# Column scans of a four-layer convolution kernel: inputs copied to contiguous lines by GpSimd, biases added when results are kept, a longer lead of one chain over the other

## The chip, the core and the metric

The kernel runs on one core of a Trainium2 chip. The metric is device time in microseconds (us) of one execution. The engines of the core work beside each other, each through its own queue in order: TensorE (PE in the profile; its weight loads are PEld), VectorE (DVE), ScalarE (ACT), GpSimd (POOL) and SyncE (SP), which issues nearly all transfers between main memory and the on-chip memory SBUF. Matmul results arrive in PSUM, which VectorE and ScalarE read.

## The reference

The input is 4 images of 48 channels and 256 x 256 pixels. Four residual layers follow each other, each on a group-normalised input: an attention layer, a gated layer, and two equal scan layers. The change is in the scan layers:

```python
def step(w, b):
    def f(carry, inp):
        nxt = inp + _conv1d(carry, w, b)
        return (nxt, nxt)
    return f
xs = jnp.moveaxis(x, 2, 0)
d0 = xs[0]
_, d_rest = jax.lax.scan(step(down_w, down_b), d0, xs[1:])
...
x = x + _L2_conv_ref(_gn(x), ...)
x = x + _L3_conv_ref(_gn(x), ...)
```

A layer makes four scans over the whole image: down over the rows, up over the rows (with the same weights, over what down gave), right over the columns and left over the columns. One step takes the line computed before, convolves it with 5 taps over all 48 channels, adds a bias and adds the next line of the scan's input. So each step needs the result of the step before it: 255 steps a scan, four scans a layer, two layers. At the end the layer's input is added to the result of left.

## The kernel before

**Tiling of the scans.** The four images make two pairs. Each pair is one *chain* (`chain`, from L1015), a generator that yields after each step. Two neighbouring pixels of a line and 48 channels fill 96 partitions; the 5 taps become three 96 x 96 matrices (j = 0, 1, 2). A line of one image is then 128 elements on 96 partitions. The newest line is the *carry*, a tile of 96 x 2 x 130 with one image in each half; four such tiles are used in turn (`NC`, L1018).

**One step** (`step`, L1037 to L1056). For each of the two images: three matmuls on the old carry into one PSUM bank (L1045), then one VectorE add of PSUM and the input line into the new carry, then `after`, which is the scan's `keep`. In the row scans (`split` true) the add is a plain one (L1049), and input and result stand in rows cut into blocks of 8 columns. In the column scans it is a `scalar_tensor_tensor` (L1053) that adds PSUM, the bias (a column of `b_sb`) and `inp`. The float32 matmul appears in the profile as two records, so that a step has 12 records on PE, 2 adds on VectorE and 2 keeps.

**Where lines lie.** A *slot* is 16 KB a partition; each pair has five, used in rotation (L996, L1012). A slot of columns holds 16 columns (`CB`) of both images in the view of `cols_view` (L1061): batch, q, h, 8 columns. One column there, `col = cols_view(column)[:, :, w % 2, :, w // 2]` (L1225), is 128 elements with a distance of 8 elements between them.

**The scans of a layer** (`layer_of`, L1080):
- down (L1113): rows from `x`, normalised by ScalarE (L1102); keep adds the bias for the next use on ScalarE (L1125) and writes the row back; blocks of 32 rows go out to `D`.
- up (L1141): blocks come back from `D`; keep is a ScalarE copy in place (L1166); results go out to `U`, laid out by column blocks (L1198).
- right (L1216): a block of 16 columns comes from `U` one block ahead (L1221); the first column is copied to the carry (L1231); keep is a ScalarE copy into the same column (L1228); the finished block goes out to `R` (L1236).
- left (L1244): blocks come back from `R` (L1249), with the layer's input `x` in a slot `stage` (L1250); keep is a GpSimd add of the carry to `stage` (L1258), and `stage` goes out (L1267). In the first scan layer VectorE takes statistics of the finished `stage`, 8 `bn_stats` for a block of 16 columns, one after each step of the next block (`late`, L1271); they give the next layer's normalisation.

**Order of the two chains.** The loops at the end of `scans` (L1349 to L1373) write chain 0 alone for `lead` yields, then both in turn until chain 0 has ended, then chain 1 alone. `LEAD` is 3 H = 768 (L27). While chain 1 is alone, `to_rows` (L1313) brings the finished output back to rows in pieces: one piece every 24 yields for pair 0, then, in the last 128 yields, one every 10 for half of pair 1. A piece is either a set of loads (L1324) or copies on GpSimd (L1340) and ScalarE (L1344) with a store (L1346). The framework's scheduler makes the final order of each engine's queue when the program is built, from that order, from priorities and from what its own timing expects to be ready. So instructions of chain 1 may be laid down earlier than the loops write them. An engine works its queue strictly in that order.

Of the kernel before, what the change touches and what calls it, by code (L numbers as in the profile page):

```python
# [19 lines left out]
P = 96  # L20
# [3 lines left out]
RT = 32  # L24
KC = 8
NK = W // (2 * KC)
LEAD = 3 * H  # L27
F = 8
GN_EPS = 1e-5
LN_EPS = 1e-5  # L30
# [934 lines left out]
def scans(ctx, tc, xs, out, wts, biases, dram, k, coefs, lead, spare):  # L965
# [49 lines left out]
    def chain(pair):  # L1015
# [8 lines left out]
        def slot(name):  # L1024
            return take(pair, f"{name}{pair}")
# [4 lines left out]
        def advance():  # L1030
            at[0] = (at[0] + 1) % NC
            return inner()

        def blocks(v):
            return v.rearrange("p b (k w) -> p b k w", w=KC)

        def step(layer, way, inp, after, split):  # L1037

            old = carry[at[0]]
            new = advance()  # L1040
            for i in range(2):
                b = slice(i, i + 1)
                ps = sums[pair].tile([P, 512], F32, tag="bank", name=f"ps{pair}{i}")[:, : W // 2]
                for j in range(3):
                    nc.tensor.matmul(  # L1045
                        ps, lhsT=w_sb[layer][:, way, j, :], rhs=old[:, i, j : j + W // 2], start=j == 0, stop=j == 2
                    )
                if split:
                    nc.vector.tensor_add(  # L1049
                        new[:, i].rearrange("p (k w) -> p k w", w=KC), ps.rearrange("p (k w) -> p k w", w=KC), inp[:, i]  # L1050
                    )
                else:
                    nc.vector.scalar_tensor_tensor(  # L1053
                        new[:, i], ps, b_sb[layer][:, way : way + 1], inp[:, i], ALU.add, ALU.add
                    )
                after(new, b)  # L1056

        def rows_view(t):
# [1 line left out]

        def cols_view(t):  # L1061
            return t.rearrange("p (b q h w) -> p b q h w", b=2, q=2, w=KC)

        def row(ts, r):
            return rows_view(ts[r % 2])[:, :, :, r // 2, :]
# [14 lines left out]
        def layer_of(layer, first):  # L1080
# [32 lines left out]
            for n in range(NT):  # L1113
                ahead_ = None
                for r in range(RT):
                    if r == 0 and n + 1 < NT:
                        ahead_ = [slot("dn"), slot("dn")]
                        load_rows(layer, n + 1, ahead_, 0, NK)
                    if ahead_ and r >= RT // 2 and r % 4 == 0:
                        i = (r - RT // 2) // 4  # L1120
                        norm(ahead_, i // 2, i % 2)
                    inp = row(now, r)

                    def keep(new, b):
                        nc.scalar.activation(inp[:, b], blocks(new[:, b]), AF.Identity, bias=bias[:, 0:1])  # L1125

                    if n == 0 and r == 0:
                        keep(inner(), slice(0, 2))
                    else:
                        step(layer, 0, inp, keep, True)  # L1130
# [10 lines left out]
            for n in reversed(range(NT)):  # L1141
                ahead_ = None
                for r in reversed(range(RT)):
# [19 lines left out]
                    place = row(now, r)  # L1163

                    def keep(new, b):
                        nc.scalar.copy(place[:, b], blocks(new[:, b]))  # L1166

                    if i == H - 1:
                        keep(inner(), slice(0, 2))
                    else:  # L1170
                        step(layer, 0, place, keep, True)
                    yield
                    if n == 0 and r < 2:

# [7 lines left out]
                if n == 0:  # L1182

                    def keep(new, b):
                        nc.scalar.copy(last[:, b], new[:, b])

                    step(layer, 0, blocks(last), keep, True)
                    yield
                    for q in range(2):
                        nc.sync.dma_start(cols_view(column)[0:C, :, q, 0, :], last[q * C : (q + 1) * C, :, 0:KC])  # L1190
# [18 lines left out]
                now = ahead_  # L1209


            for _ in range(3):
                yield
            x, y = xs[layer][pair], xs[layer + 1][pair]
            stage = None
            for n in range(NK):  # L1216
                ahead_ = None
                for w in range(CB):
                    if w == 0 and n + 1 < NK:
                        ahead_ = slot("col")  # L1220
                        nc.sync.dma_start(by_batch(ahead_), block_of(U, n + 1))  # L1221
                    if w == 0 and n + 1 == NK:
                        stage = slot("stage")
                        nc.sync.dma_start(by_batch(stage), block_of(x, n))
                    col = cols_view(column)[:, :, w % 2, :, w // 2]  # L1225

                    def keep(new, b):
                        nc.scalar.copy(col[:, b], new[:, b])  # L1228

                    if n == 0 and w == 0:  # L1230
                        nc.vector.tensor_copy(advance(), col)  # L1231
                    else:
                        step(layer, 1, col, keep, False)
                    yield
                if ahead_ is not None:
                    nc.sync.dma_start(Rt[n], column)  # L1236
                    column = ahead_


# [4 lines left out]
            for n in reversed(range(NK)):  # L1244
                ahead_ = None
                for w in reversed(range(CB)):
                    if w == CB - 1 and n > 0:
                        ahead_ = slot("col"), slot("stage")
                        nc.sync.dma_start(ahead_[0], Rt[n - 1])  # L1249
                        nc.sync.dma_start(by_batch(ahead_[1]), block_of(x, n - 1))  # L1250
                    if layer == 0 and n == 0 and w == CB // 2:
                        following = [slot("dn"), slot("dn")]
                        load_rows(1, 0, following, 1, NK)
                    col = cols_view(column)[:, :, w % 2, :, w // 2]
                    to = cols_view(stage)[:, :, w % 2, :, w // 2]

                    def keep(new, b):
                        nc.gpsimd.tensor_add(to[:, b], to[:, b], new[:, b])  # L1258

                    if n == NK - 1 and w == CB - 1:  # L1260
                        keep(inner(), slice(0, 2))
                    else:
                        step(layer, 2, col, keep, False)
                    if late:
                        late.pop(0)()
                    yield
# [12 lines left out]
                                    cols_view(stage)[r * C : (r + 1) * C, :, q, :NH, :].rearrange("c b h w -> c b (h w)"),  # L1279
                                )  # L1280
                if ahead_:
                    column, stage = ahead_
            if layer == 0:

                ends = []
# [74 lines left out]
    for _ in chains[1]:  # L1360
        i += 1
        if i < lead - W // 2:
            if i % 24 == 0:
                next(pieces, None)
        elif i == lead - W // 2:
            for _ in pieces:
                pass
            pieces = to_rows(1, NK // 2, NK // 2, [0])
        elif i % 10 == 0:
            next(pieces, None)  # L1370
# [127 lines left out]
```

## Time and profile before

| | |
|---|---|
| median of 3 runs | 9303.49 us (9290.49 to 9321.5) |
| profiled execution, own time | 9302.44 us |
| its span, first to last instruction | 9300.7 us |
| PE busy | 8807.2 us, 95% of the span |
| PE weight loads | 7274.7 us, 78% |
| DVE busy | 4378.6 us, 47% |
| ACT busy | 3355.6 us, 36% |
| POOL busy | 1454.7 us, 16% |
| moved by DMA | 1440.82 MB, mean 155 GB/s |
| granted TensorE clock, mean | 0.975 of full speed |

All times below are counted from the span's start. The span has five stretches, by where the adds of each chain start and end in the trace:

| stretch | us |
|---|---|
| attention and gated layer, with the first steps of pair 0 from 3239 | 0 to about 3520 |
| pair 0 alone: down, up, right and the start of left (with a few steps of pair 1) | to about 4650 |
| both pairs interleaved | to 7942 |
| pair 1 alone in the second scan layer: up, right (8303 to 8694), left (8694 to 9137) | to 9137 |
| last output pieces | to 9301 |

A group line of the profile gives the source line, the engine, the operation, result and inputs, size and count, then busy time and mean duration, then the engine's idle time just before and what ended it. Matmuls are pipelined and their ends are modelled, so a PE that is busy all the time may still be slower than it could be; how many matmuls a window holds shows that.

### The profile page before, as it was taken

What the parts mean: (1) busy time and instruction counts of PE and PEld (TensorE: products, weight loads), DVE (VectorE), ACT (ScalarE), POOL (GpSimd) and SP (SyncE); (2) the same over time, 40 slices, a digit from 0 to 9 for tenths busy, and PEclk for the clock granted to TensorE, in tenths of its full rate; (3) what the DMA queues carried; (4) which work ended last, traced back from release to release, by engine and by line L of the source; (5) the groups of instructions that cost most, each with busy time, mean ns of one, the idle gap of its engine ahead of it and who ended that gap; (6) DMA issues with size and microseconds to landing.
All of it is one profiled execution on the core that took longest, in us unless ns stands there. A gap on an engine that the chain in (4) does not pass through costs nothing.

```text
span 9300.7 us, 160515 instructions
## 1 busy us (share of the span) xinstructions
PE 8807.2 (95%) x62920; PEld 7274.7 (78%) x62920; DVE 4378.6 (47%) x10798; ACT 3355.6 (36%) x7053; POOL 1454.7 (16%) x2866
## 2 busy tenths in 40 slices
PE   6999999989999889999999999999999999999982
PEld 5777777433333349999899999999999999989971
DVE  3331010335555564445666544555677555445541
ACT  0010000124334456545433465555333433445200
POOL 0000000001111120000133200000333333100462
PEclk9999999999999989999999999999999999999996
DMA  7653322568888868656477675654776787698899
GB/s 153 131 128 81 78 62 65 111 140 176 179 177 186 179 152 161 141 132 174 121 177 180 141 162 130 158 142 126 195 187 174 166 192 180 136 215 193 206 217 194
DMA packets 1058039, 1440.82 MB, mean 155 GB/s; under 512 B 64976, under 2 KB 981200, under 8 KB 991232
## 3 DMA queue, kind: packets, MB, share of 16 engines
q1 hardware_dynamic: 1057184, 1430.23, 67.5%
q8 instruction: 493, 8.08, 0.4%
q14 instruction: 266, 2.18, 0.1%
q0 software_dynamic: 96, 0.33, 0.0%
HBM read 837.19 MB, written 534.77 MB: 148 GB/s over the span
## 4 chain that ended last, share of the span: by engine, by line
PE 87%; DMA 6%; DVE 2%; SPq 2%; ACT 1%; issue 1%; POOL 1%; ACTq 0%; DVEq 0%; POOLq 0%
PE ps L1045 57%; PE py L581 6%; PE acc L294 5%; PE acc L295 5%; PE acc L296 4%; PE py L590 3%; DMA tok<-x 1%; PE pt L276 1%; DMA oi<-x 1%; PE ptok L751 1%; PE pout L868 1%; DMA col<-R 1%; PE ph L698 1%; ACT x1n L541 1%; DMA sx<-in_x 1%
## 5 line engine op out<-in xcount | busy, mean ns | idle before, releaser
L1045 PE MATMUL ps<-carry,w 96*96 96x128 f32 x48960 | 5585.1, 275 | 95.2 <-DVE carry L1053 63.3
L1045 PEld LDWEIGHTS ps<-carry,w 96*96 96x96 f32 x48960 | 5446.1, 163 | 239.5 <-DVE carry L1053 95.9
L1053 DVE SCALAR_TENSOR_TENSOR carry<-ps,b,col 96x128 f32<-96x128 f32 x4080 | 1778.1, 439 | 1129.3 <-PE ps L1045 963.1
L1258 POOL TENSOR_TENSOR stage<-stage,carry 96x128 f32<-96x128 f32 (+1 forms) x2044 | 1054.9, 520 | 3809.4 <-DVE carry L1053 3629.4
L1228 ACT COPY col<-carry 96x128 f32<-96x128 f32 x2040 | 859.9, 425 | 979.6 <-DVE carry L1053 979.0
L1125 ACT ACTIVATE dn<-carry,b 96x128 f32<-96x128 f32 (+1 forms) x2044 | 790.7, 399 | 1064.7 <-DVE carry L1049 1062.1
L1049 DVE TENSOR_TENSOR carry<-ps,dn 96x128 f32<-96x128 f32 x2280 | 651.6, 287 | 748.9 <-PE ps L1045 582.4
L1049 DVE TENSOR_TENSOR carry<-ps,up 96x128 f32<-96x128 f32 x1792 | 516.5, 288 | 657.9 <-ACT up L1166 493.9
L1166 ACT COPY up<-carry 96x128 f32<-96x128 f32 x1792 | 530.8, 298 | 584.0 <-DVE carry L1049 567.1
L581 PE MATMUL py<-x1n,wy 128*96 128x512 f32 x1536 | 700.8, 605 | 29.6 <-ACT x1n L541 27.9
L295 PE MATMUL acc<-xs,xt 128*96 128x288 f32 x2048 | 667.2, 408 | 0.0
L294 PE MATMUL acc<-xt 128*96 128x288 f32 x2048 | 666.8, 409 | 0.0
L581 PEld LDWEIGHTS py<-x1n,wy 128*96 128x96 f32 x1536 | 243.7, 165 | 451.0 <-issue 434.4
L279 DVE COPY xt<-pt 128x384 f32<-128x384 f32 x256 | 136.7, 554 | 851.1 <-PE pt L276 645.5
L296 PE MATMUL acc<-xt,xs 128*96 128x192 f32 x2048 | 502.0, 327 | 0.0
L261 ACT ACTIVATE xn<-raw,coef 96x2048 f32<-96x2048 f32 x64 | 133.6, 2094 | 987.4 <-PE pt L276 819.8
L296 PEld LDWEIGHTS acc<-xt,xs 128*96 128x96 f32 x2048 | 332.4, 165 | 154.5 <-issue 1.8
L295 PEld LDWEIGHTS acc<-xs,xt 128*96 128x96 f32 x2048 | 332.2, 165 | 151.4 <-issue 2.8
L604 DVE TENSOR_TENSOR y<-py,t 96x512 f32<-96x512 f32 x256 | 171.4, 678 | 591.0 <-PE py L590 591.0
L590 PE MATMUL py<-x2n,wy 64*96 64x512 f32 x1536 | 363.0, 601 | 0.0
L294 PEld LDWEIGHTS acc<-xt 128*96 128x96 f32 x2048 | 330.8, 165 | 5.3 <-issue 1.1
L590 PEld LDWEIGHTS py<-x2n,wy 64*96 64x96 f32 x1536 | 116.9, 159 | 233.7 <-issue 231.1
(177 smaller groups left out, 4175.9 us busy)
## 6 DMA issues: line engine op xcount, KB each, us to landing
stage<-x SPq DMA_DIRECT2D x64, 1536.0 KB
x<-stage SPq DMA_DIRECT2D x64, 1536.0 KB
dn<-x SPq DMA_DIRECT2D x240, 384.0 KB
R<-col SPq DMA_DIRECT2D x60, 1536.0 KB
col<-U SPq DMA_DIRECT2D x60, 1536.0 KB
col<-R SPq DMA_DIRECT2D x60, 1536.0 KB
D<-dn SPq DMA_DIRECT2D x56, 1536.0 KB
up<-D SPq DMA_DIRECT2D x56, 1536.0 KB
```

What stands on the lines that cost most here:

```text
L294: nc.tensor.matmul(acc[0], lhsT=xt[:, h + 2, :], rhs=xt[:, here, :], start=first, stop=last)
L295: nc.tensor.matmul(acc[1], lhsT=xt[:, h + 2, :], rhs=xs[:, here, :], start=first, stop=last)
L296: nc.tensor.matmul(acc[2], lhsT=xs[:, h + 2, :], rhs=xt[:, past, :], start=first, stop=last)
L581: nc.tensor.matmul(ps, lhsT=held["w"][0][:, dx], rhs=x1n[:, 2 * c : 2 * c + 2, dx : dx + W], start=dx == 0, stop=False)
L590: nc.tensor.matmul(held["ps"][q + 2 * s], lhsT=held["w"][1][here, dx], rhs=x2n[here, 2 * q : 2 * q + 2, dx : dx + W], start=False, stop=dx ...
L1045: nc.tensor.matmul(ps, lhsT=w_sb[layer][:, way, j, :], rhs=old[:, i, j : j + W // 2], start=j == 0, stop=j == 2)
L1049: nc.vector.tensor_add(new[:, i].rearrange("p (k w) -> p k w", w=KC), ps.rearrange("p (k w) -> p k w", w=KC), inp[:, i])
L1053: nc.vector.scalar_tensor_tensor(new[:, i], ps, b_sb[layer][:, way : way + 1], inp[:, i], ALU.add, ALU.add)
L1125: nc.scalar.activation(inp[:, b], blocks(new[:, b]), AF.Identity, bias=bias[:, 0:1])
L1166: nc.scalar.copy(place[:, b], blocks(new[:, b]))
L1228: nc.scalar.copy(col[:, b], new[:, b])
L1258: nc.gpsimd.tensor_add(to[:, b], to[:, b], new[:, b])
```

## The change

Five things are changed in the scans.

1. **Input columns of right come as contiguous lines.** `fetch` lets GpSimd copy one column of both images (96 x 256) from the block into one of four line buffers, three steps before the step that adds it. Two of the four buffers share their place with the statistics tiles of left.
2. **Right's result is kept in lines.** It goes to a slot of its own in `lines_view` (column, batch, h), and from there to `R` and back; left reads its inputs as lines. `stage`, to which left adds, keeps its old view.
3. **Biases are added when a result is kept.** The keeps of up and right are ScalarE activations with the bias of the next scan, in place of plain copies; the add on VectorE is then a plain one for all four scans. The first column of right has the bias taken off again as it is copied to the carry, and is kept as a line, too.
4. **The lead** of pair 0 is 4 H - 32 = 992 yields in place of 768.
5. **Pieces of pair 0's output** come every 32 yields in place of every 24.

```diff
@@ -24,7 +24,7 @@
-LEAD = 3 * H
+LEAD = 4 * H - 32
...
-        def step(layer, way, inp, after, split):
+        def step(layer, way, inp, after):
 
             old = carry[at[0]]
             new = advance()
@@ -1045,14 +1045,12 @@
                     nc.tensor.matmul(
                         ps, lhsT=w_sb[layer][:, way, j, :], rhs=old[:, i, j : j + W // 2], start=j == 0, stop=j == 2
                     )
-                if split:
+                if len(inp.shape) == 4:
                     nc.vector.tensor_add(
                         new[:, i].rearrange("p (k w) -> p k w", w=KC), ps.rearrange("p (k w) -> p k w", w=KC), inp[:, i]
                     )
                 else:
-                    nc.vector.scalar_tensor_tensor(
-                        new[:, i], ps, b_sb[layer][:, way : way + 1], inp[:, i], ALU.add, ALU.add
-                    )
+                    nc.vector.tensor_add(new[:, i], ps, inp[:, i])
                 after(new, b)
...
+        def lines_view(t):
+
+            return t.rearrange("p (w b h) -> p w b h", w=CB, b=2)
...
                     def keep(new, b):
-                        nc.scalar.copy(place[:, b], blocks(new[:, b]))
+                        nc.scalar.activation(place[:, b], blocks(new[:, b]), AF.Identity, bias=bias[:, 1:2])
...
                     def keep(new, b):
-                        nc.scalar.copy(last[:, b], new[:, b])
-
-                    step(layer, 0, blocks(last), keep, True)
+                        nc.scalar.activation(last[:, b], new[:, b], AF.Identity, bias=bias[:, 1:2])
+
+                    step(layer, 0, blocks(last), keep)
...
+            fetched = {}
+
+            def fetch(block, n, w):
+                g = n * CB + w
+                tag = (f"st{pair}0", f"st{pair}1", f"pre{pair}0", f"pre{pair}1")[g % 4]
+                t = wp.tile([P, 2, W // 2], F32, tag=tag, name="pre")
+                nc.gpsimd.tensor_copy(t, cols_view(block)[:, :, w % 2, :, w // 2])
+                fetched[g] = t
+
+            for w in range(1, 3):
+                fetch(column, 0, w)
             for n in range(NK):
                 ahead_ = None
                 for w in range(CB):
@@ -1222,18 +1236,28 @@
                     if w == 0 and n + 1 == NK:
                         stage = slot("stage")
                         nc.sync.dma_start(by_batch(stage), block_of(x, n))
-                    col = cols_view(column)[:, :, w % 2, :, w // 2]
+                    if w == 0:
+                        lines = slot("lines")
+                    if w + 3 < CB:
+                        fetch(column, n, w + 3)
+                    elif ahead_ is not None:
+                        fetch(ahead_, n + 1, w + 3 - CB)
+                    line = lines_view(lines)[:, w]
 
                     def keep(new, b):
-                        nc.scalar.copy(col[:, b], new[:, b])
+                        nc.scalar.activation(line[:, b], new[:, b], AF.Identity, bias=bias[:, 2:3])
 
                     if n == 0 and w == 0:
-                        nc.vector.tensor_copy(advance(), col)
+
+                        nc.vector.tensor_scalar(
+                            advance(), cols_view(column)[:, :, 0, :, 0], bias[:, 1:2], None, ALU.subtract
+                        )
+                        keep(inner(), slice(0, 2))
                     else:
-                        step(layer, 1, col, keep, False)
+                        step(layer, 1, fetched.pop(n * CB + w), keep)
                     yield
                 if ahead_ is not None:
-                    nc.sync.dma_start(Rt[n], column)
+                    nc.sync.dma_start(Rt[n], lines)
                     column = ahead_
 
...
-                        ahead_ = slot("col"), slot("stage")
+                        ahead_ = slot("lines"), slot("stage")
                         nc.sync.dma_start(ahead_[0], Rt[n - 1])
...
-                    col = cols_view(column)[:, :, w % 2, :, w // 2]
+                    line = lines_view(lines)[:, w]
...
-                        step(layer, 2, col, keep, False)
+                        step(layer, 2, line, keep)
...
-                    column, stage = ahead_
+                    lines, stage = ahead_
...
         i += 1
         if i < lead - W // 2:
-            if i % 24 == 0:
+            if i % 32 == 0:
                 next(pieces, None)
```

More of the change, by code (lines that the diff above doesn't have):

```diff
@@ L1129, in layer_of @@
                     else:
-                        step(layer, 0, inp, keep, True)
+                        step(layer, 0, inp, keep)
                     yield
@@ L1170, in layer_of @@
                     else:
-                        step(layer, 0, place, keep, True)
+                        step(layer, 0, place, keep)
                     yield
```

## The prediction

> **What bounds the kernel now.** First the chain that ended last and the costliest groups of the page:
>
> ```profile
> PE 87%; DMA 6%; DVE 2%; SPq 2%; ACT 1%; issue 1%; POOL 1%; ACTq 0%; DVEq 0%; POOLq 0%
> ...
> L1045 PE MATMUL ps<-carry,w 96*96 96x128 f32 x48960 | 5585.1, 275 | 95.2 <-DVE carry L1053 63.3
> ...
> L1053 DVE SCALAR_TENSOR_TENSOR carry<-ps,b,col 96x128 f32<-96x128 f32 x4080 | 1778.1, 439 | 1129.3 <-PE ps L1045 963.1
> ...
> L1049 DVE TENSOR_TENSOR carry<-ps,dn 96x128 f32<-96x128 f32 x2280 | 651.6, 287 | 748.9 <-PE ps L1045 582.4
> ```
>
> TensorE's scan matmuls (L1045) carry the chain. 48960 records over 4080 steps (2040 for each pair) are 12 for a step, 6 for each of its two images. After its 6, an image waits for one add on VectorE: 439 ns in the column scans, 287 in the row scans. Whether that matters depends on the stage, so I read those matmuls in windows: a row scan alone, a column scan alone, both pairs interleaved, then pair 1's right scan, left scan, and left scan beside the output pieces.
>
> ```profile
> core 0: us, PE busy (x) PEld busy (x), PEclk, DMA share, GB/s
> 3900.00:4180.00 280.00, 279.09 (x2478) 276.74 (x2476) 1.00 0.60 138
> 4250.00:4590.00 340.00, 338.31 (x2710) 305.26 (x2709) 1.00 0.58 152
> 5400.00:5900.00 500.00, 500.00 (x4573) 499.97 (x4572) 1.00 0.65 143
> 8350.00:8680.00 330.00, 330.00 (x2649) 299.12 (x2647) 1.00 0.78 192
> 8700.00:8880.00 180.00, 180.00 (x1443) 163.50 (x1441) 1.00 0.81 214
> 8890.00:9136.00 246.00, 196.83 (x1488) 179.58 (x1487) 0.88 0.99 220
> ```
>
> Time divided by count, times 12, is a step. Interleaved it is 1.312 us, and weight loads fill the window (499.97 of 500): the floor. A row scan alone takes 1.356, a column scan alone 1.506, 1.495 and 1.497, call it 1.50. Busy PE is near 100% in all of these; only the count tells them apart. The model fits: a lone image needs 0.656 us for its neighbour's 6 matmuls, then hand-overs and its own add. 1.356 less 0.656 less 0.288 leaves 0.41 for the hand-overs; with 0.439 the sum is 1.505. Alone, the add is on the path; interleaved, the other pair covers it. The last window is another matter: DMA share 0.99, 220 GB/s, TensorE idle for 49 us. Transfers bound it.
>
> **Part 1: the column add.** It loses the bias pointer and reads lines instead of every eighth element. This row is nearest:
>
> ```profile
> L1053 DVE SCALAR_TENSOR_TENSOR carry<-ps,b,col x4080: 364/440/459, 4199.9 to 9136.3; 96x128 f32<-96x128 f32 x195
> ...
> L1049 DVE TENSOR_TENSOR carry<-ps,last x8: 288/288/290, 4193.2 to 8297.7; 96x128 f32<-96x128 f32 x8
> ```
>
> The second is a plain add of a PSUM bank and a contiguous 128-element line, exactly the new form. So 288 ns, and a lone column step becomes 1.356. Ends: 440 (nothing gained) and 224, the shortest row add, at which a step meets the floor; I take 288. By the built order of TensorE's queue before, pair 0 runs alone through right and 30 steps of left, pair 1 through right and left. Pair 1's last 128 left steps are bound by transfers, so 255+30+255+127 = 667 steps gain 1.503 - 1.356 = 0.147: **-98 us**. Interleaved steps gain nothing.
>
> **Part 2: GpSimd's copies.** One 96x256 copy a right step, 1020 in all. Nearest rows:
>
> ```profile
> L1258 POOL TENSOR_TENSOR stage<-stage,carry 96x256 f32<-96x256 f32 x4 | 3.4, 858 | 2457.2 <-DVE carry L1053 2430.7 <-ACT dn L1102 26.5
> ...
> L266 POOL COPY ends<-xn 96x256 f32<-96x256 f32 x8 | 3.1, 394 | 0.0
> ```
>
> Between 394 (contiguous) and 858 (two inputs, strided); nearer the copy, so about 450. Against 1.356 us a step alone, or two copies in 2.62 interleaved, it hides, even at 858. A buffer is filled three steps ahead, 4.1 us. What could uncover it is GpSimd's queue: in pair 1's last right scan the output copies (L1340, 1162 ns) stand among the fetches, at most two in a row (2.3 us), and they wait for their own loads. Before, GpSimd waited 10.8, 11.2 and 15.7 us between the halves of a group there; the new order puts 7 to 18 fetches between them, 9 to 24 us. If such a wait isn't covered, the next add waits too, and with it TensorE: six waits of up to 8 us, 0 to +48. I take +5.
>
> [...]
>
> **Part 3: biases added in the keep.** ScalarE's up keep goes from 298 (L1166 copy) to about 400 (L1125 with bias), right's stays near 424. The add waits for the keep of four steps earlier (ring of four carries), 5 us back: 0; ScalarE is 36% busy. The first column's subtraction replaces a 386 ns copy; its keep runs beside. R goes out from its own slot, same bytes: 0.
>
> **Part 4: the lead.** In the built orders pair 1's tail alone grows from 764 to 987 steps, and pair 0 is alone to step 1020 instead of about 795. The extra 223 row steps and 225 left steps cost 1.356 - 1.312 = 0.044 each: **+20**. Three further costs:
> - Pair 0's left scan of the first layer is now alone, with 8 statistics instructions a block on VectorE (L1271, 684 ns). Before, the other pair covered them. Each stands between two adds whose gap is 0.37 to 0.40 us, so it delays the next by 0.25 to 0.3, 8 a block, 15 blocks: 34. Pair 1's one step a block stands just there and fills part. Ends 0 and 36; I take **+20**.
> - The start. Before, pair 0 had 24 steps between the last normalisation of the gated layer and pair 1's first step; pair 1's first add came at 3563.3, 44 us after the last output DMA was issued (3519.7). In the new order pair 1's first 8 steps stand ahead of pair 0's step 33, so TensorE waits for pair 1's first rows with nothing else to do. The last output comes about 10 us earlier, without pair 0's steps 33 to 37 (3501 to 3514) in its way; a load then takes 25 to 40 us. At 3590 before, 85 steps were done; now about 34 by 3542, and 51 at 1.36 end at 3611. Ends 0 and +40; I take **+24**.
> - Left now runs beside left: two blocks of 4.72 MB (R and x in, y out) each 16 step pairs, 9.44 MB in 42 us, 225 GB/s. The window at 8700 moved 214 at share 0.81, so 264 fits: **+5** for edges.
>
> Output pieces come every 32 steps, not 24. The 12.9 us hole in pair 1's last up scan (8153) should mostly go: **-10**. The last 128 left steps carry the same 55 MB: 251 us before, at best 245: **-6**.
>
> Here the clock matters. After such a hole the trace shows:
>
> ```profile
> 8964.47 0.78 DVE L1053 SCALAR_TENSOR_TENSOR carry<-ps,b,col 96x128 f32<-96x128 f32 x2 [7.98 <-DMA col<-R]
> 8966.66 0.44 DVE L1053 SCALAR_TENSOR_TENSOR carry<-ps,b,col 96x128 f32<-96x128 f32 x1 [1.41 <-PE ps L1045]
> 8967.94 0.43 DVE L1053 SCALAR_TENSOR_TENSOR carry<-ps,b,col 96x128 f32<-96x128 f32 x1 [0.84 <-PE ps L1045]
> ```
>
> Adds 1.28 us apart, not 0.75, and granted clock 0.88 in the window. [...]
>
> **Sum**: -98 + 5 + 20 + 20 + 24 + 5 - 10 - 6 = -40. From the profiled execution's 9302.4 (span 9300.7, 1.7 around it; 1 below the median of 9303.5): **9262 us**, 0.4% faster. What a measurement can tell from no change is about 0.3%, 28 us.
>
> **Rivals.**
> - *The lead costs nothing* (start and statistics covered): -40 - 44, 9218. For: the scheduler may place pair 1's steps in the gaps better than I read. Against: TensorE works its queue in order.
> - *Transfers bind left beside left.* If 214 GB/s is a ceiling, a block pair takes 44.1 us, not 42: 16 x 2.1 = +34, and +4 in the tail: 9300. Decides below 225. For: no long window exceeds 220. Against: share 0.81 at 214.
> - *The add stays long*, because the time is not in stride and pointer: then 892 lone column steps (255 x 4 - 128) stay at 1.50. Part 1's 98 go and the 225 new ones cost 0.147 more, +33: 9262 + 131 = 9393, **slower**. Decides from an add of about 0.33. Against: the eight 288 rows.
> - *GpSimd becomes the bound*, from a copy of 1.31 us. At 1.6: 510 x 0.24 alone and some 210 x 0.58 beside each other: +245, 9507, **slower**. Against: 858 at most.
>
> Chances: forecast 0.60 (its own range 9215 to 9305, four fifths of it faster than 0.3%), lead free 0.16, transfers 0.14, add 0.05, GpSimd 0.05. Faster: 0.48 + 0.16 + 0.04 = 0.68. Slower: 0.10 + 0.02 = 0.12. Same: 0.20. The range takes the forecast, the free lead and the transfers: 9190 to 9315; the short end is an add of 224.
>
> **What would show it.** L1053 in the new profile as a plain add at 288 ns; lone right steps at 12 records in 1.356 us; GpSimd's copy under 0.86 us; TensorE idle for 20 to 40 us near 3520 to 3550; statistics between the adds of pair 0's lone left scan, about 24 us a block; left beside left at 42 us a block. Wrong: lone column steps still at 1.50, VectorE waiting for GpSimd in right, or TensorE waiting for R where both run left.

## The result, and the profile after

| | before | after |
|---|---|---|
| median | 9308.53 us (9290.49 to 9321.5, 6 runs) | 9266.13 us (9263.67 to 9275.03, 6 runs) |
| span of the profiled execution | 9300.7 us | 9261.9 us |
| VectorE busy | 4378.6 us | 3774.1 us |
| GpSimd busy | 1454.7 us | 2108.1 us |

The ratio is 0.9956 (95% interval 0.9943 to 0.9969). The chain's shares and the costliest groups of the page of after, as they were shown of before:

```profile
PE 86%; DMA 6%; DVE 3%; SPq 2%; POOL 1%; issue 1%; ACT 1%; ACTq 0%; DVEq 0%; POOLq 0%
...
L1045 PE MATMUL ps<-carry,w 96*96 96x128 f32 x48960 | 5495.6, 275 | 143.4 <-DVE carry L1053 109.1
...
L1225 POOL COPY pre<-col 96x256 f32<-96x256 f32 x1020 | 656.7, 645 | 2754.2 <-DMA col<-last 1969.5
...
L1053 DVE TENSOR_TENSOR carry<-ps,pre 96x128 f32<-96x128 f32 x2040 | 587.3, 288 | 797.7 <-PE ps L1045 546.7
...
L1053 DVE TENSOR_TENSOR carry<-ps,lines 96x128 f32<-96x128 f32 x2040 | 576.6, 286 | 755.6 <-PE ps L1045 640.9
```

The column add is down from 439 ns to 288 in right (input `pre`) and 286 in left (`lines`). VectorE loses 604 us of busy time, and the kernel only 39 us of its span. Which steps were waiting for the add is read from the matmuls in windows (start and end, length, PE busy with its records, granted clock, DMA share, GB/s): pair 0's up, right and left scan alone, the pairs beside each other with both in left, then pair 1's right, left, and second half of left.

```profile
core 0: us, PE busy (x), PEclk, DMA share, GB/s
3900.00:4180.00 280.00, 280.00 (x2499) 1.00 0.63 145
4220.00:4560.00 340.00, 340.00 (x2971) 1.00 0.53 143
4600.00:4940.00 340.00, 334.19 (x2939) 1.00 0.82 215
...
7000.00:7500.00 500.00, 500.00 (x4571) 1.00 0.79 219
8320.00:8650.00 330.00, 318.75 (x2753) 0.98 0.82 206
8680.00:8830.00 150.00, 150.00 (x1340) 1.00 0.77 211
8839.00:9118.00 279.00, 187.61 (x1531) 0.82 0.93 210
```

Twelve records are a step. Right alone is now at 340/2971 x 12 = 1.373 us (1.50 before), pair 1's left alone at 1.343, and interleaved steps stay at 1.313. In the last row TensorE is idle for 91 us; before, it was idle for 49 in its 246.

To place the time, I count the adds of both pairs from one landmark to the next and take 1.3123 us, the interleaved step, from the elapsed time for each. What remains is the excess of a stretch:

| stretch | before | after | change |
|---|---|---|---|
| 3480 us to the end of pair 0's first down | 51.9 | 72.5 | +20.6 |
| pair 0, up | 11.4 | 8.5 | -2.9 |
| pair 0, right | 50.5 | 16.6 | -33.9 |
| pair 0, left (after: alone) | 10.6 | 22.0 | +11.4 |
| pair 0's second layer, beside pair 1 | 28.4 | 22.7 | -5.7 |
| pair 1, second down (after: alone) | - | 19.1 | +19.1 |
| pair 1, second up | 22.2 | 11.3 | -10.9 |
| pair 1, second right | 61.5 | 37.6 | -23.9 |
| pair 1, left, first 127 steps | 23.7 | 4.3 | -19.4 |
| last 128 left steps, and what follows (us in full) | 416.2 | 423.1 | +6.9 |

The changes add up to -38.7, against 38.8 between the spans. The three lone column stretches gain 77 us; half of that is lost again: at the start, in the two stretches in which a pair now runs alone for longer, and at the end.

### The profile page after: what moved, and what is told of

It reads as the page before. It is cut to its first block, busy times and chain, and to the rows that moved or that the text cites. A ratio compares the mean times of both kernels' runs of the same rounds, so it can differ in the third digit from the quotient of the medians.

```text
span 9261.9 us, 162499 instructions
## 1 busy us (share of the span) xinstructions
PE 8718.4 (94%) x62920; PEld 7269.3 (78%) x62920; DVE 3774.1 (41%) x10798; ACT 3511.9 (38%) x7057; POOL 2108.1 (23%) x3886
## 4 chain that ended last, share of the span: by engine, by line
PE 86%; DMA 6%; DVE 3%; SPq 2%; POOL 1%; issue 1%; ACT 1%; ACTq 0%; DVEq 0%; POOLq 0%
PE ps L1045 57%; PE py L581 6%; PE acc L294 5%; PE acc L295 5%; PE acc L296 4%; PE py L590 3%; DMA tok<-x 2%; PE pt L276 1%; DMA lines<-R 1%; PE pout L868 1%; PE ph L698 1%; PE ptok L751 1%; DMA oi<-x 1%; DMA sx<-in_x 1%; POOL stage L1282 1%
## 5 line engine op out<-in xcount | busy, mean ns | idle before, releaser
L1045 PE MATMUL ps<-carry,w 96*96 96x128 f32 x48960 | 5495.6, 275 | 143.4 <-DVE carry L1053 109.1
L1225 POOL COPY pre<-col 96x256 f32<-96x256 f32 x1020 | 656.7, 645 | 2754.2 <-DMA col<-last 1969.5
L1248 ACT ACTIVATE lines<-carry,b 96x128 f32<-96x128 f32 (+1 forms) x2044 | 815.7, 401 | 614.9 <-DVE carry L1053 611.1
L1127 ACT ACTIVATE dn<-carry,b 96x128 f32<-96x128 f32 (+1 forms) x2044 | 768.7, 398 | 705.9 <-DVE carry L1049 703.0
L1053 DVE TENSOR_TENSOR carry<-ps,pre 96x128 f32<-96x128 f32 x2040 | 587.3, 288 | 797.7 <-PE ps L1045 546.7
L1168 ACT ACTIVATE up<-carry,b 96x128 f32<-96x128 f32 x1792 | 718.4, 402 | 481.9 <-DVE carry L1049 480.8
L1053 DVE TENSOR_TENSOR carry<-ps,lines 96x128 f32<-96x128 f32 x2040 | 576.6, 286 | 755.6 <-PE ps L1045 640.9
```

The lines of the kernel that those rows point to most:

```text
L1045: nc.tensor.matmul(ps, lhsT=w_sb[layer][:, way, j, :], rhs=old[:, i, j : j + W // 2], start=j == 0, stop=j == 2)
L1053: nc.vector.tensor_add(new[:, i], ps, inp[:, i])
L1168: nc.scalar.activation(place[:, b], blocks(new[:, b]), AF.Identity, bias=bias[:, 1:2])
L1225: nc.gpsimd.tensor_copy(t, cols_view(block)[:, :, w % 2, :, w // 2])
L1248: nc.scalar.activation(line[:, b], new[:, b], AF.Identity, bias=bias[:, 2:3])
```

## The experiments

The theory I began with: the column add brings the gain, and the longer lead takes about 40 us of it back, partly at the start. The rivals: the lead is free; or the start is late for another reason. The runs fall into several comparisons, each with the kernel before timed beside it; its median moved from 9304 to 9311 us between them, so a difference of some 7 us between runs of different comparisons says nothing alone, and the stretches of the traces carry the argument.

**1. The change with the old lead, and the old kernel with the new lead.**

```diff
-LEAD = 4 * H - 32
+LEAD = 3 * H
...
-            if i % 32 == 0:
+            if i % 24 == 0:
```

> The changed kernel with the lead back at 768 yields and a piece every 24; all else of the change is kept. If the longer lead costs what the prediction's sum says (20 for lone steps, 20 for statistics between lone adds, 5 at block edges, less 10 gained by sparser pieces), this runs about 35 us shorter than the changed kernel: 9225 to 9240. The early steps of pair 1 stand ahead of pair 0's step 33 here too, so the start stays as slow as in the changed kernel. The rival, that the lead is what gains (equal scans beside each other, sparser pieces), expects 9280 or more.

Measured: 9227.27 us (9224.45 to 9232.02), ratio 0.9918 (0.9904 to 0.9932). The reverse edit was made to the kernel before:

> The kernel before with the lead of 992 and a piece every 32, nothing else of the change. If lone column steps at 1.50 us are what the longer lead pays for, 225 more of them cost 225 x 0.19 = 43 us over the interleaved floor, 223 lone row steps 8 to 10, statistics between lone adds up to 20, less 10 for sparser pieces: 9360 to 9375. The rival that the lead gains by itself expects less than 9303.

Measured: 9375.88 us (9367.2 to 9379.48), ratio 1.0076 (1.0062 to 1.009), at the upper end of what was expected. So the lead, with its sparser pieces, costs about 39 us with the fast add and 71 with the slow one (9304.48 in the same comparison); with the old lead the rest of the change is worth 77 us. Against the run with the old lead, pair 0's lone left and pair 1's lone down cost 20 and 19 us more in after, pair 1's up 12 less, and the last stretch 12 more (423.1 against 411.4). The start, however, is late with either lead: its excess was 75.3 us with 768. The new lead isn't its cause.

**2. The start: pair 1 held back.** The prediction had TensorE wait because pair 1's first steps stand ahead of pair 0's step 33 in its queue. Here pair 1's first normalisation is made to wait for pair 0's step 64.

```diff
+                    if pair == 0 and layer == 0 and n == 2 and r == 0:
+                        held.append(wp.tile([P, 1], F32, tag="held", name="held"))
+                        nc.vector.tensor_scalar_mul(held[0], inner()[:, 0, 0:1], 0.0)
...
+                own = g[:, 1:2]
+                if pair == 1 and layer == 0:
+                    own = home.tile([P, 1], F32, tag=f"own{b}", name="own")
+                    nc.vector.tensor_add(own, g[:, 1:2], held[0])
+                    nc.vector.tensor_add(t[:, 1:2], t[:, 1:2], held[0])
...
```

> The changed kernel with pair 1's first normalisation made to wait for a value of pair 0's step 64 (a zero that is added to its bias), so that pair 1's first steps can't stand ahead of pair 0's step 33 in TensorE's queue. If the start costs 24 to 26 us because TensorE waits in order for pair 1's rows, this is 24 to 30 us shorter than the changed kernel: 9236 to 9242, and the idle stretch of TensorE near 3520 to 3560 is gone. If the start is slow for another reason (transfers or ScalarE at the end of the gated layer), it stays within 8 us of 9266.

Measured: 9280.45 us (9272.72 to 9284.97), ratio 0.9972 (0.9961 to 0.9982). Neither came. Pair 1 was out of the way (its first add came at 4208 us), and pair 0's step 33, the first that needs row 33, still came at 3555.8 us, where it came at 3556.2 in after; TensorE was busy for 3.6 us between 3520 and 3560. The theory of the queue falls: pair 0 waits for something of its own. The run is slower than after because pair 1's first steps no longer fill the hole: in after TensorE was busy for 20.8 of the same 40 us.

What it waits for is in VectorE's waits between 3440 and 3620 us (line waited for, us in total, times, longest), first with pair 1 held back (L1110 is the same line as L1104 of after), then in after:

```profile
DVE carry L1049 <- ACT dn L1110: 29.6, 2, 29.1
```

```profile
DVE carry L1049 <- ACT dn L1104: 18.8, 2, 18.4
```

The 29.1 us are pair 0's step 33. The 18.4 us of after are pair 1's first step, at 3541.8: TensorE does wait there for pair 1's rows, as the prediction says, but pair 1's eight steps end at about 3556, and pair 0's rows are normalised no sooner (ScalarE ends at 3556.0). SyncE's queue in after (start and us of a group of issues, line, transfer, count):

```profile
3478.98 0.47 SPq L889 DMA_DIRECT2D x<-y  x1
3479.50 6.46 SPq L1136 DMA_DIRECT2D D<-dn  x1
3494.36 3.47 SPq L850 DMA_DIRECT2D xr<-x  x4
3497.87 0.47 SPq L889 DMA_DIRECT2D x<-y  x1
3498.39 8.76 SPq L1075 DMA_DIRECT2D dn<-x  x3
3513.99 0.30 SPq L889 DMA_DIRECT2D x<-y  x1
3514.39 4.73 SPq L1008 DMA_DIRECT2D w<-in_c3w  x1
3519.17 1.08 SPq L1010 DMA_DIRECT2D b<-in_c3b  x1
3520.30 55.61 SPq L1075 DMA_DIRECT2D dn<-x  x27
```

L1104 is the normalisation of a block's rows. By the built program, the loads of the second tile of pair 0's block 1, which holds row 33, are among the 27 issues after 3520 (from 3533 to 3540): they stand behind the gated layer's last output (L889), the scan's weights and pair 1's first loads. In the kernel before they were issued from 3463 to 3487. Nothing in the diff moves them. But the new line buffers `pre` lie in the pool `c_w`, which is opened before most of the tile slots; a longer `c_w` moves those slots in SBUF. By the addresses of the built programs, that tile lay at bytes 109504 to 125888 of a partition before and lies at 113600 to 129984 in after, where its end overlaps `xt`, a tile of the gated layer, from 128896. By the trace TensorE reads `xt` for the last time at 3457.6 us, so the overlap alone doesn't hold the loads until 3533. The scheduler laid them that far back in the queue; by what in its own timing stays open. Whether the position of the buffers decides it can be tested.

**3. The line buffers in a pool of their own, opened last**, with the new lead and with the old one.

```diff
     slots_d = pool("c_slot_d", 5)
+    pre_p = pool("c_pre", 1)
...
-                t = wp.tile([P, 2, W // 2], F32, tag=tag, name="pre")
+                t = (wp if tag[0] == "s" else pre_p).tile([P, 2, W // 2], F32, tag=tag, name="pre")
```

> The changed kernel with the two new line buffers of each pair in a pool of their own that is opened last; the statistics' buffers stay where they were. Theory (the new buffers lengthen a pool that lies ahead of the tile slots, so the second tile of pair 0's block 1, with row 33 in it, is loaded 50 us later, behind the gated layer's last outputs): pair 0's step 34 starts at 3500 to 3510 us again instead of 3561, the excess from 3480 us to the end of pair 0's first down scan falls from 72 to about 50 us, and the time from 9266 to 9240 to 9248 us. Rival (the late start belongs to the longer lead or to the order in which pair 1 is started): step 34 stays near 3561 us and the time at 9262 to 9270 us.

> The same edit with the lead back at 768 steps (pieces every 24 steps). If the start and the lead are two separate costs, their gains add: 39 us for the lead and 20 to 26 us for the start off 9266 us, 9200 to 9210 us. If the two are one cost, no better than the lead alone: 9222 to 9232 us.

Measured: 9256.14 us (9249.67 to 9259.01), ratio 0.9943 (0.9931 to 0.9956), and with the old lead 9207.07 (9205.15 to 9214.45), ratio 0.9893 (0.988 to 0.9907). SyncE's queue with the buffers moved (new lead; line numbers are one higher) has the loads back before the last output:

```profile
3484.51 0.47 SPq L889 DMA_DIRECT2D x<-y  x1
3485.02 7.51 SPq L1076 DMA_DIRECT2D dn<-x  x2
3498.20 3.47 SPq L850 DMA_DIRECT2D xr<-x  x4
3501.71 0.47 SPq L889 DMA_DIRECT2D x<-y  x1
```

Step 34 begins at 3507 us (3559 in after), and with the old lead at 3499, as the theory said. Counted from step 32, which shifts by up to 8 us between these executions, the start gains 21 and 24 us. The tile lies at its old place again. Not every growth of `c_w` makes the start late: in the run of experiment 5 the pool grows by half as much, the tile ends at 127936, short of `xt`, and step 34 begins at 3505 us. Of all 14 programs here, step 34 begins between 3558 and 3564 us in the five whose tile reaches `xt`, and between 3498 and 3518 in the others. The time of the second run is in its range; the first gained 10 us where 18 to 26 were expected. Its profiled execution reached step 32 5.6 us later than that of after, and pair 0's up and right were 6 us longer than there in excess (11.2 and 20.0). Why these two follow the early start (they do so in each run that has it) stays open.

**4. Which part of the change shortens the add.** The kernel before with the biases in the keeps, without GpSimd's copies and without lines: a plain add, still of every eighth element.

```diff
-                    nc.vector.scalar_tensor_tensor(
-                        new[:, i], ps, b_sb[layer][:, way : way + 1], inp[:, i], ALU.add, ALU.add
-                    )
+                    nc.vector.tensor_add(new[:, i], ps, inp[:, i])
...
-                        nc.scalar.copy(col[:, b], new[:, b])
+                        nc.scalar.activation(line[:, b], new[:, b], AF.Identity, bias=bias[:, 2:3])
...
```

> The kernel before with the biases added when results are kept, and nothing else: the column add is a plain one, but still reads every eighth element; lead 768, no copies, no lines. It splits the 152 ns between pointer and stride. If all of it is the pointer form, the add takes 288 and lone column steps 1.35: about 9210 to 9225. If it is the stride, the add stays near 440 and the time at 9300. The prediction's reading (72 ns for the pointer by the 512-element rows, the rest stride) gives an add of about 365, a lone step of 1.43 and 667 x 0.07 = 47 us: 9255.

Measured: 9267.71 us (9258.97 to 9272.16), ratio 0.996 (0.9946 to 0.9973). Its group:

```profile
L1053 DVE TENSOR_TENSOR carry<-ps,col 96x128 f32<-96x128 f32 x2160 | 817.9, 379 | 677.0 <-PE ps L1045 653.8
```

So the bias operand is worth 60 ns of the add and the distance between elements 92. (The 72 ns of the expectation come from two instructions of 512 elements in the kernel before, 750 ns with such an operand and 678 without, which the prediction doesn't show.) That ScalarE now writes every eighth element beside the add is not what lengthens it: in left, where ScalarE keeps nothing, the add took 381 ns in the median. A lone column step was 1.44 us. This small part of the change, with the old lead and no new buffers, is as fast as the whole of it as it stands; with the old lead and an early start (experiment 3) the whole is 60 us faster.

**5. The 29 ns that right has more than left.** A lone left step takes 1.346 us in the median, a lone right step 1.375, with the same add. In right VectorE waits for GpSimd's copy as well. Is it the wait, or do the copies disturb VectorE's reads? One copy for two columns has as many elements, and makes the wait needed only every other step (with the old lead; the copy comes two steps ahead):

```diff
-                tag = (f"st{pair}0", f"st{pair}1", f"pre{pair}0", f"pre{pair}1")[g % 4]
-                t = wp.tile([P, 2, W // 2], F32, tag=tag, name="pre")
-                nc.gpsimd.tensor_copy(t, cols_view(block)[:, :, w % 2, :, w // 2])
+                tag = (f"st{pair}0", f"st{pair}1")[g // 2 % 2]
+                t = wp.tile([P, 2, 2, W // 2], F32, tag=tag, name="pre")
+                nc.gpsimd.tensor_copy(t.rearrange("p q b h -> p b q h"), cols_view(block)[:, :, :, :, w // 2])
...
```

> Lead 768, and GpSimd's copy takes two neighbouring columns at a time into two buffers of double size (no new tags, the statistics' buffers grow in their place, and the start's loads are early as in the run beside it). Theory (the first add of each right step starts 29 ns late because VectorE takes a third wait, on GpSimd): every other step has no such wait, a lone right step falls from a mean of 1.375 to about 1.36 us, some 510 such steps make 7 to 8 us less than the run beside it, 9193 to 9203 us if that one gives 9200 to 9210. Rival (the copy slows VectorE's reads by contention): the same elements are copied, the mean stays at 1.375 us and the time within 3 us of the run beside it; if a copy of twice the length is late for the first of its two columns, slower than the run beside it by up to 20 us.

Measured: 9207.83 us (9199.24 to 9221.12), ratio 0.9894 (0.988 to 0.9907), no different from the run beside it. VectorE in pair 0's right scan (start, duration, idle before it in brackets), first in after, then in this run with one of GpSimd's copies ahead of the adds:

```profile
4400.70 0.29 DVE L1053 TENSOR_TENSOR carry<-ps,pre 96x128 f32<-96x128 f32 x1 [0.46 <-ACT lines L1248]
4401.33 0.29 DVE L1053 TENSOR_TENSOR carry<-ps,pre 96x128 f32<-96x128 f32 x1 [0.34 <-PE ps L1045]
4402.08 0.29 DVE L1053 TENSOR_TENSOR carry<-ps,pre 96x128 f32<-96x128 f32 x1 [0.46 <-ACT lines L1248]
```

```profile
4401.23 1.11 POOL L1225 COPY pre<-col 96x512 f32<-96x512 f32 x1 [1.61 <-DVE carry L1053]
...
4401.52 0.29 DVE L1053 TENSOR_TENSOR carry<-ps,pre 96x128 f32<-96x128 f32 x1 [0.43 <-ACT lines L1249]
4402.15 0.29 DVE L1053 TENSOR_TENSOR carry<-ps,pre 96x128 f32<-96x128 f32 x1 [0.34 <-PE ps L1045]
4402.87 0.29 DVE L1053 TENSOR_TENSOR carry<-ps,pre 96x128 f32<-96x128 f32 x1 [0.43 <-ACT lines L1249]
4403.53 0.29 DVE L1053 TENSOR_TENSOR carry<-ps,pre 96x128 f32<-96x128 f32 x1 [0.37 <-PE ps L1045]
4404.25 0.29 DVE L1053 TENSOR_TENSOR carry<-ps,pre 96x128 f32<-96x128 f32 x1 [0.43 <-ACT lines L1249]
```

Each step has two adds, and only the first carries the wait on GpSimd. (The profile names ScalarE's keep as what ended that add's idle time; by the program the add waits for the keep of four steps before, which was done long ago.) In after every step is 1.375 us. In the second fence steps of 1.35 and 1.38 us alternate (medians over the scan 1.346 and 1.375), while the add is 0.29 us throughout. The second add of the step at 4401.52 starts while the same copy still runs (until 4402.34), and isn't late with 0.34 us before it; the 0.37 of the step after I read as the first add's delay, handed on by TensorE's order. So it is the wait. Pair 0's and pair 1's right scans had 5.9 and 1.7 us less excess than in the run beside it, the 7 to 8 expected; the start of this execution happened to be about 6 us longer. In the times this is too little to see.

**6. The statistics of the lone left scan, done twice** in the changed kernel.

```diff
-                    late += [lambda b=b, c=c, f=stat: f(b, c) for b in range(2) for c in range(4)]
+                    late += [lambda b=b, c=c, f=stat: f(b, c) for b in range(2) for c in (range(4) if pair else (0, 0, 1, 1, 2, 2, 3, 3))]
```

> The changed kernel with every one of pair 0's statistics of the first layer's left scan (128 instructions of 680 ns on VectorE, one after a step) done twice: it computes the same. Theory (a statistic between two lone adds delays the next one by some 0.16 us, 20 us in all, as the prediction priced them): 128 more cost 15 to 25 us, 9281 to 9291 us, and a block of 16 lone steps 23.6 us becomes 24.6 to 25.2. Rival (pair 1's one step per block fills what the statistics open, or they fit in VectorE's idle time): at most 5 us, 9264 to 9271 us, the block stays at 23.6 to 23.9 us.

Measured: 9253.35 us (9249.16 to 9253.92), ratio 0.9939 (0.9923 to 0.9956): faster than after, where slower was expected. In the scan itself a block of 16 steps went from 23.57 to 24.54 us, 0.12 us for each statistic, and the scan from 376.3 to 390.5 us, 14 where 15 to 25 were expected. But the longer generator of pair 0 put pair 1 eight steps on, and the first output piece of pair 1's last left scan fell 8 steps later. The last 128 steps and what follows them took 398.2 us instead of 423.1. The miss led to the last cause.

**7. Where the output pieces fall.** First in the changed kernel, moved by four steps:

```diff
-        elif i % 10 == 0:
+        elif (i - lead) % 10 == 2:
```

> The changed kernel with its lead of 992 steps, and only the steps at which pair 1's output pieces are issued in the last left scan moved by 4: first 10 steps after the middle instead of 6, 12 pieces instead of 13, as it falls with a lead of 768. Theory (the last 128 left steps and what follows them take 423 us with the long lead and 411 with the short one because of this phase): 411 to 415 us, the time 9253 to 9259 us. Rival (the sum of bytes and their rate fix this stretch whatever the phase): 420 to 425 us, 9263 to 9269 us.

Measured: 9255.63 us (9251.7 to 9264.41), ratio 0.9945 (0.9931 to 0.9958), the last stretch at 412.3 us. Then with the old lead, the buffers moved, and the first piece 14 steps after the middle:

```diff
-        elif i % 10 == 0:
+        elif i % 10 == 4 and i > lead - W // 2 + 10:
```

> Lead 768, line buffers in their own pool (9207 us before this edit), and the first piece of the last left scan's second half 14 steps after its middle instead of 10; 12 pieces either way. In the runs so far the last 128 left steps and what follows them took 423 us with the first piece 6 steps after the middle, 411 to 412 with 10, and 398 with 14 (the run with doubled statistics). Theory (the first piece's loads wait for the last left blocks to be stored, and what stands behind them in SyncE's queue waits too): 397 to 402 us here, the time 9193 to 9199 us. Rival (the 398 us had to do with the doubled statistics, or with the long lead): 410 to 414 us, 9204 to 9211 us.

Measured: 9196.35 us (9191.69 to 9199.21), ratio 0.9882 (0.9866 to 0.9899), the last stretch at 396.6 us. The window view of this stretch, of after and of this run, has the length, the clock, the DMA share and the rate:

```profile
8838.80:9261.90 423.10, 0.72 0.92 201
```

```profile
8793.30:9189.90 396.60, 0.73 0.97 215
```

201 x 423.1 and 215 x 396.6 are both 85 MB: the bytes are the same, and the DMA engines stand idle less. With pieces from step 6, 10 and 14 the stretch took 423 to 430, 411 to 415 and 397 to 398 us in the runs with the fast add. From 6 to 10 one piece of 13 drops out of the scan; from 10 to 14 the number stays. That it is a matter of place is shown; which transfer waits for which is not settled (the waits of SyncE's queue do not line up with the times over these runs).

**8. The pieces before that**, with the old lead and the buffers moved: at steps 8 and 16 of each 24, not 0.

> Lead 768 with the line buffers in their own pool, and pair 0's output pieces at steps 8, 32, 56 ... of pair 1's last scans instead of 0, 24, 48 ... Theory (the hole of 14 us in pair 1's last up scan comes because a piece's store waits 20 us for ScalarE's copy at the head of SyncE's queue, ahead of the loads of the next rows): whether that happens is a matter of where the pieces fall, so this phase or the other one of the pair (16) loses the hole: 9192 to 9197 us; the phase that doesn't, 9204 to 9211 us. Rival (the hole is the price of so many bytes in this scan, wherever they fall): both phases 9204 to 9211 us.

> The same with the pieces at steps 16, 40, 64 ...: 9192 to 9197 us if the hole is gone in this phase, 9204 to 9211 us if not.

Measured: 9208.09 us (9201.27 to 9225.35) and 9218.8 (9212.34 to 9225.01), ratios 0.9895 (0.988 to 0.991) and 0.9904 (0.9889 to 0.9918); 9207.07 without the edit. At 8 the hole of 14 us left pair 1's up scan (excess 26.9 to 11.2 us), and right grew by 11 (34.9 to 45.5), since its first column now waited 10.8 us for a transfer in place of 2.7; at 16 it was 19 us, at another place of up. (The profiled execution at 8 is 17 us above that run's median; it was 19 us late before the scans' step 33 already, which the edit doesn't touch.) With 24 steps between pieces, moving them moves the hole and doesn't remove it.

## Why the prediction came out as it did

The time was 9266 where 9262 was predicted, and the spans differ by 38.8 us where 40 were. The sum is right; several of its terms are not, and their errors cancel, which is luck.

- **Column add, 440 to 288 ns: right; the gain of 98 us: too large.** The row of eight plain adds gave the new duration exactly. The lone column step was taken as 1.356 us, that of a row step; left reached 1.346, right 1.375. The three lone stretches gained 77 us instead of 98. The prediction reads a lone column step as 1.50 us and then takes 1.503; with 1.50 the term is 96. It missed what the prediction's own Part 2 added: a wait for GpSimd in each right step. That costs 29 ns against left, and 1.375 against 1.356 is 10 us over the 510 lone steps. Further, pair 0's share of left (30 steps) is counted with its lone left scan here, and the wait named next lies in pair 1's right.
- **GpSimd's copy, 450 ns: mis-sized, without effect.** It took 645 ns, within the bounds of 394 and 858, and fits a step of 1.37. Its queue cost +5 in the prediction, for output copies ahead of it. VectorE waited for a copy three times in pair 1's last right scan, 13.6 us in all and 11.4 in one; the copy in turn waited for its block of columns, not for output copies. From after's waits between 8300 and 8345 us:

```profile
POOL pre L1225 <- DMA col<-U: 15.5, 1, 15.5
DVE carry L1053 <- POOL pre L1225: 11.4, 1, 11.4
```

  Before, VectorE waited for that block itself, 6.9 us. The increase is 5 to 7 us: the size is right, the cause another. VectorE's adds were hardly longer beside GpSimd's work. In the kernel before, the column add took 437 ns with GpSimd idle (452 adds in 197.31 us, 4250 to 4590) and 442 with GpSimd busy for 126 of 180 us (240 in 106.06, 8700 to 8880). In after it took 288 with GpSimd copying for 154 of 340 us (4220 to 4560), and, in the run of experiment 5, adds start on time beside copies of 1111 ns.
- **Biases in the keeps: right**, 402 ns for up's keep, and no waits that count.
- **The start, +24: right in size, wrong in mechanism.** It measured +20.6. Of the 24, 3611 less 3590 gives 21; the other 3, meant for slower steps behind the wait, no run shows as a cost of its own. In after the granted clock was 0.50 until 3548 us and 1.00 from 3550, and the first seven gaps between pair 1's adds took 8.8 us (3541.8 to 3550.6), the next seven 4.7; two of the first seven hold, by the profile, waits for row loads (1.74 and 1.75 us). The step that failed is "pair 1's first 8 steps stand ahead of pair 0's step 33, so TensorE waits for pair 1's first rows": they did, and it waited until 3541.8 us, close to the 3542 of the prediction, but with pair 1 out of the way pair 0's step 33 came no sooner (experiment 2). It waited for row data whose load had moved behind the last outputs, because the small new buffers moved its slot (experiment 3). The order of TensorE's queue was read, that of SyncE's for the same rows was not. That the two waits end within 14 us of each other, and so the size agrees, is luck.
- **Lone steps and statistics, +40: right in sum**, 39 against the run with the old lead (20 and 19). Within it the statistics cost less than 20: a block took 23.57 us, where 16 lone steps and one of pair 1 are 16 x 1.346 + 1.31 = 22.85, so 0.7 a block or 11 us. A wait for late normalised rows in pair 1's down scan, 7.8 us near 7900, had not been foreseen and made up for it, by luck.
- **Left beside left, +5: nothing.** 4571 records in 500 us are the floor, at 219 GB/s and share 0.79: 42 us for 16 step pairs, as worked out. This also ends the rival of bound transfers there.
- **Sparser pieces, -10: right in size** (pair 1's up, -10.9). The hole did go, and unlike in experiment 8 right did not grow for it (37.6 us with pieces every 32 steps, 37.3 with the old lead). The edit changes distance and place of the pieces at once; which of the two removes the hole is not shown.
- **The last 128 left steps, -6: wrong.** They took 279 us, not 245, where the kernel before needed 252; the tail behind them fell from 164 to 144, so that both together took 6.9 us more. The step that failed is "carry the same 55 MB: 251 us before, at best 245": it takes bytes and rate as fixed. In after 58 MB moved in these steps, and over steps and tail the rate ran from 201 to 215 GB/s with where the pieces fall (experiment 7).

Of the other rivals, a free lead (9218) is refuted by 39 us, the long add by 288 ns, and GpSimd as the bound by 645 ns against 1.31 us. The granted clock in the kernel before was 0.50 from 8964 to 8968 us, right behind the hole that the prediction shows, and 1.00 from 8970 to 8972; the rows of after have it at 0.82 where TensorE is idle for a third of the time and at 0.98 to 1.00 elsewhere.

## What to carry to other kernels

A faster instruction pays only in the stretches where it ends a wait (here VectorE lost 604 us of busy time, the span 39): count those steps first, and look for a cheap part of the change that gives as much as the whole bundle (here the bias moved into the keep, without copies, buffers or a new lead). When a change adds even a small buffer, compare the transfer queue as well as the engines' queues, since a moved allocation can put a load behind work it had nothing to do with (here loads issued from 3533 us, where they were issued from 3463). And test each part of a bundle alone: here the old lead, buffers out of the way and output pieces four steps later gave 9196 us, 1.2% under the kernel before and 70 us under the bundle.

## What the runs showed of the hardware

- A VectorE add of PSUM and a 128-element float32 line took 288 ns from a contiguous line, 379 from elements 8 apart, and 439 with a bias column as a third operand besides.
- One more wait in a step, on GpSimd's copy, cost 29 ns, although nowhere in pair 0's right scan was that copy the last thing VectorE waited for.
- GpSimd's copy of 96 x 256 float32 took 645 ns from elements 8 apart, and 394 in the contiguous copy that the prediction showed; 512 elements took 1111.
- ScalarE's keep with bias took 401 ns into a contiguous line and 528 into elements 8 apart (experiment 4).
